# Smaller attention blocks, finer row work in the first search, and longer turns in the quantile stage of a graph-attention and quantile kernel

## The chip, the cores and the metric

The kernel runs on one core of one Trainium2 chip. The metric is the device time of one launch in microseconds (us), the median of several runs. Engines are named as in the profile: PE (TensorE), DVE (VectorE), ACT (ScalarE), POOL (GpSimd), SP (SyncE). PEld is PE's weight load.

## What is computed

Two layers over the same graph of 4096 nodes with 128 features each. `adj` is a 4096 x 4096 matrix of 0 and 1 with about 32 neighbours per row (11 to 55 with these inputs). The first layer is graph attention with eight heads, an output product, elu, a residual and a layer norm. The second takes, for each node, half of its neighbours by a rule on their positions, and of these the quantiles 0.25, 0.5 and 0.75 in each feature.

```python
# layer 0
Wh = jnp.einsum('nd,hde->hne', nodes, W)
f1 = jnp.einsum('hnd,hd->hn', Wh, a1)
f2 = jnp.einsum('hnd,hd->hn', Wh, a2)
e = jax.nn.leaky_relu(f1[:, :, None] + f2[:, None, :], negative_slope=ALPHA)
att = jnp.where(mask, e, jnp.float32(-9000000000000000.0))
att = jax.nn.softmax(att, axis=-1)
h = jax.nn.elu(jnp.einsum('hnm,hmd->hnd', att, Wh))
cat = jnp.transpose(h, (1, 0, 2)).reshape(N, NHEADS * DIM)
x = jax.nn.elu(cat @ W1 + b1)
out = _layernorm(nodes + x, gamma, beta)
# layer 1
m_i = jnp.where(num_nbr > T, jnp.ceil(num_nbr / K).astype(jnp.int32), jnp.int32(1))
remove = mask & ((rank + 1) % skip[:, None] == 0)
keep = mask & ~remove
svals = jnp.sort(jnp.where(keep[:, :, None], x[None, :, :], big), axis=1)
for q in QUANTILES:
    idx = jnp.maximum(jnp.ceil(q * n_keep).astype(jnp.int32) - 1, 0)
    agg = agg + w_q * jnp.take_along_axis(svals, idx[:, None, None], axis=1)[:, 0, :]
agg = (1.0 - SELF_RATIO) * agg + SELF_RATIO * x
out = agg @ W.T + b + x
```

## The kernel before

Rows are handled in 32 tiles of 128. The work has four stages that overlap.

*Search* (`neighbours`, L624 on). For each tile the adjacency row block is loaded (two halves of 1 MB, on ACT's DMA queue, L635), ACT takes its sign (L642), PE turns 512 columns at a time into keys that grow with the column's position (two products, L681 and L684), and DVE takes the eight largest keys of each 128 columns (L648). Eight such pieces make a tile. One tile later DVE selects the 64 largest of these, eight per piece (L653, L655). Groups of three or four tiles are then completed into records (`complete_records`): the neighbours' numbers, the count, the node's own number, its f1 terms and its features.

*Node rows* (`node_rows`, L542 on). Each node's features are transposed on PE (L585), copied by ACT (L587) and multiplied with the folded attention vectors `wa` (L579), which DVE makes from `W_sb` and `a_b` (L565, L568). The features with the f2 terms are stored as rows of `xt_d` in device memory. This generator runs inside the first search: each piece of the search is followed by one step of it.

*Attention*, in blocks of `BLOCKS` tiles (6, 10, 16). Once a block's tiles are searched, its rows are ordered by their number of neighbours (`rank_by_count`), their records are scattered in that order to `rec_d` (L228, tile name `rec_d`), and read back tile by tile (`read_lists`: R at L860, `narrow` at L886, both on SP's queue). So a tile holds rows of like size, and `CAPS` says how many neighbours a tile of a block needs. Its gathers are laid out in layers: of 32 neighbours for all rows, then of 16, 8 or 4 neighbours. `LAYERS` gives, for some tiles, layers that begin at a later row group (the third number), so that only the rows with most neighbours take part. Each gather is an indirect DMA of 128 rows of `xt_d` issued by POOL (L219, tile `G`); `G` has six buffers of 16 gathers. `attend` then adds f1 and f2 (L949), takes Exp on ACT (L956), makes denominators and their spread with PE (L964, L980), scales, spreads the weights (`wide`, L999) and sums the gathered rows with PE into `y` (L1012); then follow the head product (`hT`), elu, the output product (`small`), and the norm, whose result `x_t` is scattered to `x_d` by POOL. `TURNS` is the order of tiles in a block. While a block is attended, the next block's search runs in pieces between the steps of attention, `quota` of them per tile, spread evenly over all tiles but the last. In the last block, which has no search beside it, the records of all rows are also ordered over all tiles (`all_d`) and the lists of the second layer are made.

*Quantiles* (`quantile_out`, L1168 on). For each unit (one tile or two), POOL gathers the kept neighbours' rows of `x_d` into `vals` (L219, two buffers, one unit ahead), and DVE runs a network of minima and maxima over whole rows (L1225), keeping only the places that a quantile needs (`goal`); PE sums these with weights (L1244) and makes the output, which POOL scatters (L228, `out_dram`). Between network instructions DVE copies one word from PSUM to `junk` (L1196) to end what the code calls a turn; network instructions are cut so that a turn stays within `TURN_MIN`, `TURN_AIM` and `TURN_MAX`, in us by the model `TT_FIX + elements * TT_EACH`:

```python
if then(c * m) > TURN_MAX:
    room = int((TURN_AIM - then(0)) / (size * TT_EACH))
    if ran and room < 1:
        turn_of_gpsimd()
...
ran = then(c * m)
if ran > TURN_MIN:
    turn_of_gpsimd()
```

If a row doesn't fit its tile's bounds (`bad`), a general path at the end recomputes everything; it does not run with these inputs. The order of instructions on DVE, PE, ACT and POOL is that of the program and of its generators, moved only where the framework's fixed schedule brings later ready work forward.

Of the kernel before, what the change touches and what calls it, by code (L numbers as in the profile page):

```python
# [9 lines left out]
F32 = mybir.dt.float32  # L10
# [9 lines left out]
P = 128  # L20
N = 4096
D = 128
H = 8
NT = N // P
# [17 lines left out]


CAPS = {
    6: [28, 30, 33, 35, 39, 61],
    10: [26, 28, 30, 31, 33, 34, 36, 38, 40, 61],
    16: [24, 26, 28, 29, 30, 31, 31, 32, 33, 34, 35, 36, 38, 39, 42, 62],
    32: [
        23, 24, 25, 26, 27, 27, 28, 29, 29, 30, 30, 30, 31, 31, 32, 32,
        33, 33, 34, 34, 35, 35, 36, 36, 37, 37, 38, 39, 40, 41, 44, 63,  # L50
    ],
}
BLOCKS = [6, 10, 16]


LAYERS = {
    (6, 0): [(0, 16, 0), (16, 8, 0), (24, 4, 1)],
    (6, 2): [(0, 32, 0), (32, 8, 7)],
    (6, 5): [(0, 32, 0), (32, 16, 0), (48, 16, 15)],
    (10, 0): [(0, 16, 0), (16, 8, 0), (24, 4, 2)],  # L60
    (10, 4): [(0, 32, 0), (32, 32, 31)],
    (10, 7): [(0, 32, 0), (32, 4, 0), (36, 4, 2)],
    (10, 9): [(0, 32, 0), (32, 16, 0), (48, 16, 14)],
    (16, 14): [(0, 32, 0), (32, 8, 0), (40, 4, 2)],
    (16, 15): [(0, 32, 0), (32, 16, 0), (48, 16, 14)],
}


TURNS = {6: range(6), 10: range(10), 16: [0, 1, 2, 3, 15, 4, 5, 6, *range(8, 15), 7]}

CAP = CAPS[NT]
LOW = [
# [13 lines left out]


TT_FIX, TT_EACH, TT_OVER = 0.148, 0.001042, 0.077
TURN_MIN, TURN_AIM, TURN_MAX = 1.25, 1.45, 1.7


R_NUM, R_OWN, R_F1 = L, L + 1, L + 2
# [1 line left out]
R_X = R_F1 + H  # L94
# [8 lines left out]
def layers(c):  # L103


    out = []
    s = 0
    for w in (32, 32, 16, 8, 4):
        if (c + 3) // 4 * 4 - s >= w:
            out.append((s, w, 0))  # L110
            s += w
    return out
# [130 lines left out]
def kernel(  # L243
# [18 lines left out]
    xt_d = dram.tile([N + P, XW], F32, name="xt_d")  # L262
    recs_d = [dram.tile([n * P, REC], F32, name=f"rec{n}_d") for n in BLOCKS]
    all_d = dram.tile([N, REC1], F32, name="all_d")
# [35 lines left out]
    def search(t0, n):  # L300
        return neighbours(
            tc, adjp, cp, kp, rec, num, adj, t0, n, parts, markb, oneb, bad, jp1, pidx
        )

    with tc.tile_pool(name="setup", bufs=1) as sp, tc.tile_pool(
# [15 lines left out]
        )  # L321
        iota(nc, rowi, [[1, P]])
        rows = node_rows(tc, sp, pp, rec, x, W, W_sb, a1, a2, Wl, wa, WlT, ident, bad, xt_d)
        for i, _ in enumerate(search(0, BLOCKS[0])):
            if i > 0:
# [32 lines left out]
    def prepare(b, i, t0):  # L358
        n = BLOCKS[b]
        i = TURNS[n][i]  # L360
        parts = LAYERS.get((n, i)) or layers(CAPS[n][i])
        return read_lists(tc, attp, recs_d[b], i, CAPS[n][i], parts, t0 + i, bad, narrow, nodeq)

# [41 lines left out]
    def store_records(b, t0, ranks):  # L405

        return [
            (recs_d[b], rec[:, t0 + i, :], ranks[:, i : i + 1]) for i in range(BLOCKS[b])
        ]

    t0 = 0
    with tc.manual_schedule(engines=ORDERED):
        ranks = rank_by_count(tc, cp, kp, num, jp1, before, oneb, 0, BLOCKS[0])
        for v in store_records(0, 0, ranks):
# [22 lines left out]
        )  # L437
        for b, n in enumerate(BLOCKS):
            last = b == len(BLOCKS) - 1
# [102 lines left out]
def node_rows(tc, sp, pp, rec, x, W, W_sb, a1, a2, Wl, wa, WlT, ident, bad, xt_d):  # L542


    nc = tc.nc
    c = NT // 4
    load = nc.scalar.dma_start
    load(W_sb, W.rearrange("h d e -> d h e"))
    yield
    a_b = sp.tile([P, 2, H * D], F32, name="a_b")  # L550
    for i, a in enumerate((a1, a2)):
        load(a_b[:, i, :], a.rearrange("h d -> (h d)").partition_broadcast(P))
    wl_sb = sp.tile([P, D], F32, name="wl_sb")
    load(wl_sb, Wl)
    yield
    for i in range(4):
        for _ in range(3):
            yield
        load(
            rec[:, ts(i, c), R_X : R_X + D],  # L560
            x[ts(i, c * P), :].rearrange("(t p) d -> p t d", p=P),
        )
    for i in range(2):
        wprod = sp.tile([P, H, D], F32, name="wprod")
        nc.vector.tensor_tensor(  # L565
            wprod, W_sb, a_b[:, i, :].rearrange("p (h d) -> p h d", h=H), ALU.mult
        )
        nc.vector.tensor_reduce(wa[:, ts(i, H)], wprod, AX.X, ALU.add)  # L568
        yield
    F = sp.tile([P, NT, 2 * H], F32, name="F")  # L570
    xT = f_ps = None
    for t in range(0, NT + 8, 4):
        if f_ps is not None:
            nc.scalar.copy(F[:, t - 8 : t - 4, :], f_ps)
            f_ps = None
        if xT is not None:
            f_ps = pp.tile([P, 4, 2 * H], F32, name="f_ps")
            for u in range(4):
                nc.tensor.matmul(f_ps[:, u, :], lhsT=xT[:, ts(u, P)], rhs=wa, start=True, stop=True)  # L579
            xT = None  # L580
        yield
        if t < NT:
            xt_ps = pp.tile([P, 4 * P], F32, name="xt_ps")
            for u in range(4):
                nc.tensor.transpose(xt_ps[:, ts(u, P)], rec[:, t + u, R_X : R_X + D], ident)  # L585
            xT = sp.tile([P, 4 * P], F32, name="xT", bufs=2)
            nc.scalar.copy(xT, xt_ps)  # L587
        yield
    for dst, src in ((R_F1, F[:, :, 0:H]), (R_X + D, F[:, :, H:])):
        nc.vector.tensor_scalar(rec[:, :, dst : dst + H], src, FMAX, -FMAX, ALU.min, ALU.max)  # L590
    for i in range(4):
        nc.sync.dma_start(
            xt_d[ts(i, c * P), :].rearrange("(t p) w -> p t w", p=P),
            rec[:, ts(i, c), R_X:],
        )
    pad = sp.tile([P, XW], F32, name="pad")
    nc.gpsimd.memset(pad[:, 0:D], 0.0)
    nc.gpsimd.memset(pad[:, D:], PADF)
    nc.sync.dma_start(xt_d[N:, :], pad)
    yield  # L600
    sq = sp.tile([P, NT, 2 * H], F32, name="sq")
    nc.vector.tensor_tensor(sq, F, F, ALU.mult)
    fm = sp.tile([P, NT], F32, name="fm")
    nc.vector.tensor_reduce(fm, sq, AX.X, ALU.max)

    nc.vector.tensor_scalar(fm, fm, FMAX * FMAX, None, ALU.is_le)
    nc.vector.tensor_scalar(bad[:, 3, :], fm, -1.0, 1.0, ALU.mult, ALU.add)
    yield
    wl_ps = pp.tile([P, 4 * P], F32, name="xt_ps")[:, 0:D]
    nc.tensor.transpose(wl_ps, wl_sb, ident)  # L610
    nc.scalar.copy(WlT, wl_ps)
# [886 lines left out]
```

## Time and profile before

| what | us |
|---|---|
| median of 3 runs (lowest, highest) | 3615.5 (3614.76, 3617.49) |
| profiled execution | 3611.8 |
| its span | 3610.1 |
| first gather of rows (`G`) starts | 150.8 |
| last gather of rows starts | 1778.7 |
| first gather of `vals` starts | 1828.3 |
| first and last network instruction (L1225) start | 1857.3, 3596.3 |
| busy: PE, DVE, ACT, POOL | 1258, 2743, 400, 2344 |

Starts are from the profiled execution, counted from the span's start. In the slices of the page each digit is the busy share of a 40th of the span in tenths. POOL's busy time counts the 0.94 us of an indirect DMA and not the 0.30 us to the next one, so a full row of gathers shows as 7. A group's line gives the count, the busy time, the mean time of one, and the idle time of its engine just before it with what ended it.

### The profile page before, as it was taken

The numbers are of one execution on the slowest core, as the hardware profiler recorded it, in microseconds if no ns is written. First come the engines' busy times: TensorE is split into PE (matmuls) and PEld (weight loads), VectorE is DVE, ScalarE is ACT, GpSimd is POOL, SyncE is SP. The second block draws the span as 40 slices with busy tenths as digits, with TensorE's granted clock in tenths as the row PEclk, the third lists the DMA queues.
The fourth block names the chain that finished last, engine by engine and source line by source line (L and its number), as shares of the span: only waits on it lengthen the run. The fifth ranks groups of instructions, "written<-read, shape, count | busy, mean of one in ns | idle before, by whom it ended". The sixth has DMA issues, their size and how long they took to land. (4 is left out here: it accounts for less than half of the span.)

```text
span 3610.1 us, 22900 instructions
## 1 busy us (share of the span) xinstructions
PE 1258.1 (35%) x5323; PEld 951.4 (26%) x5323; DVE 2742.8 (76%) x7591; ACT 399.5 (11%) x555; POOL 2344.3 (65%) x2341
## 2 busy tenths in 40 slices
PE   6377667878456454456610000000000000001101
PEld 3044545445455454355510000000000000000101
DVE  7787548877345122157448999999999999999998
ACT  3122122322111011111110000000000000000000
POOL 1375767757777777777557776777555766667530
PEclk9965557566556555555555555555555555555555
DMA  6443244432222222222111111111111111111100
GB/s 212 132 147 90 67 149 139 142 123 70 59 63 55 55 55 54 66 58 55 43 38 48 48 47 41 46 47 46 39 34 37 47 44 40 43 45 47 38 20 3
DMA packets 109137, 237.46 MB, mean 66 GB/s; under 512 B 46720, under 2 KB 63104, under 8 KB 100800
## 3 DMA queue, kind: packets, MB, share of 16 engines
q0 software_dynamic: 74368, 156.34, 15.5%
q10 hardware_dynamic: 14848, 70.85, 5.7%
q1 hardware_dynamic: 19776, 8.73, 1.1%
q8 instruction: 44, 0.72, 0.1%
q14 instruction: 101, 0.83, 0.1%
HBM read 224.60 MB, written 11.15 MB: 65 GB/s over the span
## 5 line engine op out<-in xcount | busy, mean ns | idle before, releaser
L219 POOL DMA_INDIRECT G<-xt_d,idx x1124 | 1096.6, 976 | 416.3 <-issue 324.0
L219 POOL DMA_INDIRECT vals<-x_d,idx x1024 | 1052.3, 1028 | 333.9 <-issue 298.0
L1225 DVE TENSOR_TENSOR work<-work 128x512 f32<-128x512 f32 (+6 forms) x1405 | 959.4, 710 | 0.4
L1244 PE MATMUL st_ps<-dg,goal 128*128 128x128 f32 x286 | 71.8, 429 | 1644.7 <-DVE goal L1225 1574.6
L1225 DVE TENSOR_TENSOR work<-work,work 128x512 f32<-128x512 f32 (+5 forms) x958 | 604.9, 655 | 0.7
L1244 PEld LDWEIGHTS st_ps<-dg,goal 128*128 128x128 f32 x286 | 63.8, 324 | 1651.0 <-issue 1650.2
L1012 PE MATMUL y<-wide,G 128*128 128x32 f32 (+3 forms) x2248 | 482.7, 392 | 26.9 <-DVE wide L999 26.9
L1012 PEld LDWEIGHTS y<-wide,G 128*128 128x128 f32 x2248 | 461.2, 309 | 62.3 <-DVE wide L999 30.0
L648 DVE MAX8 first<-key 128x8 f32<-128x128 f32 x1024 | 225.2, 281 | 119.0 <-PE key L684 118.5
L949 DVE TENSOR_TENSOR z<-G,f1x 128x128 f32<-128x128 f32 (+5 forms) x92 | 29.0, 328 | 307.9 <-DMA G<-xt_d,idx 302.7
L228 POOL DMA_INDIRECT out_dram<-o,own_i x32 | 51.0, 1593 | 295.3 <-ACT o L1270 276.1
L681 PE MATMUL key<-sgn,markb 128*128 128x512 bf16 x256 | 149.3, 583 | 145.3 <-DVE first L648 98.2
L1196 DVE COPY junk<-still 128x1 f32<-128x1 f32 x1295 | 191.2, 148 | 0.0
L1225 DVE TENSOR_TENSOR work<-vals 128x1024 f32<-128x1024 f32 (+8 forms) x140 | 138.8, 1007 | 46.2 <-DMA vals<-x_d,idx 45.9
L642 ACT ACTIVATE sgn<-adj_t 128x2048 bf16<-128x2048 int32 x64 | 122.1, 1907 | 355.4 <-PE key L681 304.8
L1043 PE MATMUL small<-W_sb,late 128*128 128x128 f32 x512 | 126.0, 430 | 88.4 <-DVE late L1040 88.4
L1243 ACT ACTIVATE dg<-ident,wt 128x128 f32<-128x128 f32 x143 | 47.5, 393 | 955.9 <-PE st_ps L1244 955.6
L964 PE MATMUL small<-z,own 128*4 128x32 f32 (+6 forms) x438 | 49.6, 280 | 284.8 <-ACT z L956 284.8
L684 PE MATMUL key<-parts,oneb 64*128 64x512 bf16 x256 | 147.2, 575 | 0.2 <-POOL parts L237 0.2
L1043 PEld LDWEIGHTS small<-W_sb,late 128*128 128x128 f32 x512 | 111.7, 324 | 102.7 <-DVE late L1040 99.0
L980 PE MATMUL rz<-rden,ownT 4*128 4x32 f32 (+6 forms) x438 | 97.8, 386 | 78.0 <-DVE rden L975 63.0
L1031 PE MATMUL hT<-late,W_sb 128*128 128x128 f32 x512 | 110.9, 385 | 35.4 <-ACT late L1025 35.4
(184 smaller groups left out, 1763.3 us busy)
## 6 DMA issues: line engine op xcount, KB each, us to landing
adj_t<-in_adj_dram ACTq DMA_DIRECT2D x64, 1024.0 KB
G<-xt_d,idx POOLq DMA_INDIRECT x1124
vals<-x_d,idx POOLq DMA_INDIRECT x1024
R<-rec_d SPq DMA_DIRECT2D x128, 26.2 KB
xt_d<-rec SPq DMA_DIRECT2D x4, 544.0 KB
rec<-in_x_dram ACTq DMA_DIRECT2D x4, 512.0 KB
narrow<-rec_d SPq DMA_DIRECT2D x68, 5.2 KB
a_b<-in_L_gnn_a_dram ACTq DMA_DIRECT2D x2, 512.0 KB
```

Of the source, the lines that this page charges most:

```text
L219: nc.gpsimd.indirect_dma_start(out=dst, out_offset=None, in_=rows, in_offset=bass.IndirectOffsetOnAxis(ap=idx, axis=0),)
L642: nc.scalar.activation(sgn, adj_t, AF.Sign, accum_out=cnt[:, i : i + 1])
L648: nc.vector.max(first[:, ts(c0 // CW + c, 8)], key[:, ts(c, CW)])
L681: nc.tensor.matmul(key, lhsT=markb, rhs=sgn[:, ts(b, 512)], start=True, stop=False)
L684: nc.tensor.matmul(key, lhsT=oneb[0:64, :], rhs=parts[1][:, ts(r - 1, 512)] if r else parts[0], start=False, stop=True)
L980: nc.tensor.matmul(rz[:, layer[i] * H : (layer[i] + w - g0) * H], lhsT=ownT[w][:, r, :], rhs=rden.rearrange("p (g r h) -> p r g h", r=k // ...
L1012: nc.tensor.matmul(yf[:, ts(g, c)], lhsT=G[:, col + j - a, 0:D], rhs=pf[:, ts(j, c)], start=(i == 0 and g % (w // 2) == w // 2 - 1), stop= ...
L1031: nc.tensor.matmul(hT[:, ts(h, P)], lhsT=consts["W_sb"][:, h, :], rhs=yT[:, h, :], start=True, stop=True)
L1043: nc.tensor.matmul(o, lhsT=hv[:, h, :], rhs=consts["W1_sb"][:, h, :], start=(h == 0), stop=(h == H - 1))
L1196: nc.vector.tensor_copy(junk, late["still"])
L1225: nc.vector.tensor_tensor(slots_of(dst, (j, c, s, m), size), slots_of(a, (i, c, s, m), size), slots_of(b, (i + d, c, s, m), size), op,)
L1244: nc.tensor.matmul(st_ps[:, u, :], lhsT=goal[:, (j * k + u) * D : (j * k + u + 1) * D], rhs=dg, start=(j == 0), stop=False,)
```

## The change

There are three parts. (1) In the first search the node rows are done one tile per step: one transpose, one copy, and the product three steps later, instead of four transposes and four products in alternate steps; the loads of W and the attention vectors are issued some steps later. (2) The bounds of a turn in the quantile stage go from 1.25, 1.45 and 1.7 to 1.1, 1.9 and 2.4. (3) The blocks are 4, 6, 9 and 13 tiles instead of 6, 10 and 16, with caps, layers and an order of turns of their own. In the kernel after, the same lines have numbers that are 7 to 10 higher.

```diff
--- before.py
+++ after.py
@@ -42,31 +42,38 @@
 
 
 CAPS = {
+    4: [29, 33, 37, 60],
     6: [28, 30, 33, 35, 39, 61],
-    10: [26, 28, 30, 31, 33, 34, 36, 38, 40, 61],
-    16: [24, 26, 28, 29, 30, 31, 31, 32, 33, 34, 35, 36, 38, 39, 42, 62],
+    9: [26, 28, 30, 32, 33, 35, 37, 40, 61],
+    13: [25, 27, 28, 30, 31, 32, 33, 34, 35, 37, 39, 41, 62],
     32: [
         23, 24, 25, 26, 27, 27, 28, 29, 29, 30, 30, 30, 31, 31, 32, 32,
         33, 33, 34, 34, 35, 35, 36, 36, 37, 37, 38, 39, 40, 41, 44, 63,
     ],
 }
-BLOCKS = [6, 10, 16]
+BLOCKS = [4, 6, 9, 13]
 
 
 LAYERS = {
+    (4, 1): [(0, 32, 0), (32, 8, 7)],
+    (4, 2): [(0, 32, 0), (32, 4, 0), (36, 8, 7)],
+    (4, 3): [(0, 32, 0), (32, 16, 0), (48, 16, 15)],
     (6, 0): [(0, 16, 0), (16, 8, 0), (24, 4, 1)],
     (6, 2): [(0, 32, 0), (32, 8, 7)],
     (6, 5): [(0, 32, 0), (32, 16, 0), (48, 16, 15)],
-    (10, 0): [(0, 16, 0), (16, 8, 0), (24, 4, 2)],
-    (10, 4): [(0, 32, 0), (32, 32, 31)],
-    (10, 7): [(0, 32, 0), (32, 4, 0), (36, 4, 2)],
-    (10, 9): [(0, 32, 0), (32, 16, 0), (48, 16, 14)],
-    (16, 14): [(0, 32, 0), (32, 8, 0), (40, 4, 2)],
-    (16, 15): [(0, 32, 0), (32, 16, 0), (48, 16, 14)],
+    (9, 0): [(0, 16, 0), (16, 8, 0), (24, 4, 2)],
+    (9, 4): [(0, 32, 0), (32, 4, 1)],
+    (9, 6): [(0, 32, 0), (32, 4, 0), (36, 4, 2)],
+    (9, 8): [(0, 32, 0), (32, 16, 0), (48, 16, 14)],
+    (13, 0): [(0, 16, 0), (16, 8, 0), (24, 4, 3)],
+    (13, 6): [(0, 32, 0), (32, 4, 2)],
+    (13, 9): [(0, 32, 0), (32, 4, 0), (36, 4, 3)],
+    (13, 11): [(0, 32, 0), (32, 8, 0), (40, 4, 3)],
+    (13, 12): [(0, 32, 0), (32, 16, 0), (48, 16, 14)],
 }
 
 
-TURNS = {6: range(6), 10: range(10), 16: [0, 1, 2, 3, 15, 4, 5, 6, *range(8, 15), 7]}
+TURNS = {4: range(4), 6: range(6), 9: range(9), 13: [0, 1, 2, 3, 12, 4, 6, 7, 8, 9, 10, 11, 5]}
 
 CAP = CAPS[NT]
 LOW = [
@@ -86,7 +93,7 @@
 
 
 TT_FIX, TT_EACH, TT_OVER = 0.148, 0.001042, 0.077
-TURN_MIN, TURN_AIM, TURN_MAX = 1.25, 1.45, 1.7
+TURN_MIN, TURN_AIM, TURN_MAX = 1.1, 1.9, 2.4
 
 
 R_NUM, R_OWN, R_F1 = L, L + 1, L + 2
@@ -545,8 +552,11 @@
     nc = tc.nc
     c = NT // 4
     load = nc.scalar.dma_start
+    for _ in range(4):
+        yield
     load(W_sb, W.rearrange("h d e -> d h e"))
-    yield
+    for _ in range(2):
+        yield
     a_b = sp.tile([P, 2, H * D], F32, name="a_b")
     for i, a in enumerate((a1, a2)):
         load(a_b[:, i, :], a.rearrange("h d -> (h d)").partition_broadcast(P))
@@ -554,7 +564,7 @@
     load(wl_sb, Wl)
     yield
     for i in range(4):
-        for _ in range(3):
+        for _ in range(2):
             yield
         load(
             rec[:, ts(i, c), R_X : R_X + D],
@@ -568,24 +578,24 @@
         nc.vector.tensor_reduce(wa[:, ts(i, H)], wprod, AX.X, ALU.add)
         yield
     F = sp.tile([P, NT, 2 * H], F32, name="F")
-    xT = f_ps = None
-    for t in range(0, NT + 8, 4):
-        if f_ps is not None:
-            nc.scalar.copy(F[:, t - 8 : t - 4, :], f_ps)
-            f_ps = None
-        if xT is not None:
-            f_ps = pp.tile([P, 4, 2 * H], F32, name="f_ps")
-            for u in range(4):
-                nc.tensor.matmul(f_ps[:, u, :], lhsT=xT[:, ts(u, P)], rhs=wa, start=True, stop=True)
-            xT = None
+
+    LAG = 3
+    turned, f_ps = [], None
+    for t in range(NT + LAG):
+        if t < NT:
+            xt_ps = pp.tile([P, 4 * P], F32, name="xt_ps")[:, 0:P]
+            nc.tensor.transpose(xt_ps, rec[:, t, R_X : R_X + D], ident)
+            xT = sp.tile([P, P], F32, name="xT", bufs=LAG + 2)
+            nc.scalar.copy(xT, xt_ps)
+            turned.append(xT)
+        u = t - LAG
+        if u >= 0:
+            if u % 4 == 0:
+                f_ps = pp.tile([P, 4, 2 * H], F32, name="f_ps")
+            nc.tensor.matmul(f_ps[:, u % 4, :], lhsT=turned.pop(0), rhs=wa, start=True, stop=True)
         yield
-        if t < NT:
-            xt_ps = pp.tile([P, 4 * P], F32, name="xt_ps")
-            for u in range(4):
-                nc.tensor.transpose(xt_ps[:, ts(u, P)], rec[:, t + u, R_X : R_X + D], ident)
-            xT = sp.tile([P, 4 * P], F32, name="xT", bufs=2)
-            nc.scalar.copy(xT, xt_ps)
-        yield
+        if u > 0 and u % 4 == 3:
+            nc.scalar.copy(F[:, u - 3 : u + 1, :], f_ps)
     for dst, src in ((R_F1, F[:, :, 0:H]), (R_X + D, F[:, :, H:])):
         nc.vector.tensor_scalar(rec[:, :, dst : dst + H], src, FMAX, -FMAX, ALU.min, ALU.max)
     for i in range(4):
```

## The prediction

> **What bounds the kernel now.** I read the page first (busy shares, slices, costliest groups), then the stretches cut where the kernel changes stage, then the waits of VectorE inside the attention stage, then the order of time in the quantile stage. The chain that ended last holds only the final stores (0.7% of the span, "issue"), so it says nothing here.
>
> ```profile
> DVE  7787548877345122157448999999999999999998
> POOL 1375767757777777777557776777555766667530
> L219 POOL DMA_INDIRECT G<-xt_d,idx x1124 | 1096.6, 976 | 416.3 <-issue 324.0
> L219 POOL DMA_INDIRECT vals<-x_d,idx x1024 | 1052.3, 1028 | 333.9 <-issue 298.0
> L1196 DVE COPY junk<-still 128x1 f32<-128x1 f32 x1295 | 191.2, 148 | 0.0
> ```
>
> ```profile
> 120.00:150.80 30.80, 3.10 (x7) 0.69 (x7) 13.59 (x58) 0.00 (x0) 8.30 (x14) 1.00 0.09 27
> 150.80:476.70 325.90, 216.50 (x773) 135.60 (x773) 215.79 (x832) 65.49 (x68) 223.35 (x230) 0.60 0.37 112
> 476.70:1005.00 528.30, 382.28 (x1585) 261.38 (x1585) 363.51 (x1336) 126.52 (x133) 369.81 (x376) 0.60 0.37 111
> 1005.00:1781.00 776.00, 425.47 (x2097) 389.52 (x2097) 316.64 (x992) 104.16 (x112) 590.62 (x604) 0.55 0.22 57
> 1828.30:3610.00 1781.70, 125.97 (x542) 108.00 (x542) 1723.93 (x3944) 58.67 (x185) 1137.51 (x1088) 0.52 0.14 40
> ```
>
> Columns of the stretches: length, then busy time and count of PE, PEld, DVE, ACT, POOL. Two limits follow each other. Up to 1828 us it is POOL's row of gathers: a gather takes 0.944 us and the next starts 0.30 later, so 1.25 us each; POOL at "7" is full. In 1005 to 1781 it does 604 operations in 776 us, 1.285 each. In the two stretches before, 230 and 376 operations take 326 and 528 us: at 1.25 that leaves some 38 and 58 us in which POOL waits. From 1828 on DVE is the limit: 1724 of 1782 us.
>
> ```profile
> DVE bad L869 <- DMA R<-rec_d: 52.4, 3, 50.4
> DVE up L867 <- DMA R<-rec_d: 39.6, 2, 38.8
> ```
>
> These are VectorE's waits in attention: at each border between blocks it stands still once (50.4 and 38.8 us) until the next block's records are stored and read back, and the next search stands with it.
>
> ```profile
> 2500.05 0.41 DVE L1225 TENSOR_TENSOR work<-work,work 128x256 f32<-128x256 f32 x1
> 2500.32 0.96 POOL L219 DMA_INDIRECT vals<-x_d,idx  x1 [0.30 <-issue]
> 2500.39 0.14 DVE L1196 COPY junk<-still 128x1 f32<-128x1 f32 x1
> ...
> 2501.58 1.03 POOL L219 DMA_INDIRECT vals<-x_d,idx  x1 [0.30 <-issue]
> 2501.72 0.14 DVE L1196 COPY junk<-still 128x1 f32<-128x1 f32 x1
> 2501.79 0.94 DVE L1225 TENSOR_TENSOR work<-work 128x768 f32<-128x768 f32 x1
> 2502.66 0.41 DVE L1225 TENSOR_TENSOR work<-work,work 128x256 f32<-128x256 f32 x1
> ```
>
> Start to start, 768 elements take 0.87 us and 256 take 0.34: 1.04 ns per element and 0.07 per instruction; the copy also costs 0.07. Both gathers end 0.89 us after the copy begins that follows their start (2501.28 and 2502.61): a gather gets through when a DVE instruction gives way to the next.
>
> **What the Trainium skill says.** "SBUF — State Buffer", Who interferes with whom: a VectorE instruction with two SBUF inputs contends with a GpSimd one that reads SBUF, and the loser waits. The trace agrees: gathers lengthen only in the quantile stage (mean 1028 against 944 ns median in attention) and end in step with VectorE. "VectorE: DVE Perf Modes", the errata section: a fixed price per instruction, not a factor, and (N+151)/0.96 ns for an fp32 sum. The trace has 682 ns for 512, as that gives 691, but overlapped starts leave only 0.07 us of it per instruction; I use the trace.
>
> **The change part by part.**
>
> *Quantile pieces (longer turns).* Running the cutting rule of both kernels over the 21 units: the network's instructions go from 2649 (the page's groups of L1225 add up to this) to 2250, turns from 1295 to 1118; elements stay 1,382,784. Check of the prices: 1,382,784 x 1.042 ns + 3944 x 0.067 = 1705 us; the trace has 1739 from the first network instruction (1857.3) to the last (3596.4), 13.8 of it a wait. So 399 + 177 = 576 instructions at 0.067 go: -38.6. Against it stands POOL: a unit's turns cover the next unit's gathers. Before, 78 turns face 66 gathers and 2 stores; after, pairs have 59 for 68, 55 for 64, 50 for 60. A copy alone would no longer be enough, but borders between two network instructions let gathers through too (2309.36 is such a border: gather 2309.30 ends at 2310.26), `vals` is free after some 10% of a unit, and a wait costs only in the last units where the lead is used up. Laying each unit's gathers along its borders (one per border, starts at least 1.2 us apart) leaves some 4 us of waits; if only the copy and the instruction after it let POOL in, 22. So -34, between -17 and -39.
>
> *First search: 4 tiles, finer node rows.* Before, the first gather of rows starts at 150.8. Read from the order of time: a piece of the search costs 1.57 us (DVE), but 2.4 while four transposes and four products share PE (two pieces 4.79); the third sign pass is 5 us late behind the `a_b` and `wl` issues on ACT's queue (2.2 and 1.57); a tile is 8 pieces; the last tile's selection takes 7.8; bookkeeping and ranks 11 (116.0 to 127.1); six scatters 2.66 apart; 8.0 from the last to the first gather. After: pieces 0 to 7 end at 19 as now; the third sign stands ahead of the loads, so piece 15 ends at 33 (8 x 1.57, 1 of wait); two pieces and the four `wprod` instructions of 1.21, 41; 14 pieces with one transpose (0.23) and one product (0.43) beside 1.06 of key products on PE, 1.72 each, 65; last selection 74; bookkeeping 11, plus 2.3 for the clamps and squares now queued on DVE ahead of the ranks, ranks at 88. Of the 35 row steps 25 fall into the search; the last 10, 0.7 each on PE, delay the ranks' products by 1 or 2 us, taken in. Four scatters instead of six: 2 x 2.66 less. First gather at 107: -43, give or take 8. ScalarE's 32 copies in place of 8 cost nothing while it idles (0.3 us each beside 1.72). The stores of `xt_d` (2.2 MB on SP's queue, ahead of the R reads) move to 84; at the 113 to 321 GB/s of the first stretches they take 7 to 20 us and 23 are there; if slower, the first gather moves with them, up to 10.
>
> *Blocks 4, 6, 9, 13 with own partial layers.* Gathers per block: before 217 + 351 + 556 = 1124, after 151 + 217 + 317 + 451 = 1136; 12 x 1.25 = +15. Two more `rec_d` scatters lie in POOL's row (28 against 26): +2.6. Bookkeeping of DVE per layer follows the lists, 66 to 71, at about 1.2 us, beside gathers. What remains is POOL's waiting: 1630 us from 150.8 to 1781 against 1211 operations at 1.285, 74 us. I walk through the new blocks with the steps that the trace shows: the Exp passes are 54.7 us apart with 20 pieces per step and 48.7 with 17, so 15 + 2 per piece; a tile's G buffers are free 36 us after its Exp (27 to 38 seen); six buffers of 16 columns. Block of 4: 21 pieces per step, Exps at 145, 202, 259; POOL reaches the fourth tile at 237 and ends near 307. Border 10 us as at 467 to 477 before. Block of 6 (18 pieces): Exps from 383 every 51; POOL waits 7, 6 and 24 us for buffers, ends near 648. Border 10. Block of 9 (16 pieces): Exps from 718 every 47; waits of 9, 16 and 21, end 1126. Last block from 1134: 451 + 32 + 13 = 496 operations at 1.285, 1771 against 1781. So the 43 us from the start shrink to -10: 18 for more operations, the rest for a third border and its buffer waits. I take -8, between -59 (waiting 40 in all) and +50. The 47 us from there to the first `vals` gather stay.
>
> **Sum.** -34 - 8 = -42. The profiled execution took 3611.8 (span 3610.1), so 3570; the median of the runs is 3.7 higher, 3615.5, so 3573.5.
>
> **The rivals.**
> - *The search no longer holds back POOL.* For: per block, steps of search are fewer per gather (62 pieces for 151, 89 for 217, 124 for 317; before 97 for 217 and 148 for 351). Waiting 40 instead of my 94: -43 + 18 - 34 = -59, with the quantiles -93: 3522. Against: 21 pieces in a step of 41 us of gathers is more than now.
> - *The longer pieces starve the gathers.* A piece of 2048 elements holds off a gather for 2.2 us; 59 turns do not serve 68. Only 17 of 38 remain: 3615.5 - 17 - 8 = 3590. Against: gathers seen ending at plain borders.
> - *The third border eats it all (slower).* POOL's 74 us of waiting over two borders are 37 each; if each of three costs 50, because the searches of 9 and 13 tiles start only after VectorE's standstill of 39 to 50 us and hold the buffers, the attention is -43 + 18 + (150 - 74) = +51; with -34, 3632. It decides from 44 per border on (132 in all). For: the two waits shown. Against: a smaller block's waits for buffers are fewer.
> - *The change does not do what it says*: a tile whose neighbours overflow its layers would start the general path. Sorting the rows' neighbour counts of these inputs (11 to 55) into the new blocks, no row exceeds its layers; left out.
>
> **How the numbers follow.** Forecast (3574, its own range 3550 to 3595) 45%; search no longer holding back (3522) 20%; starved gathers (3590) 15%; third border (3632) 13%; 7% for mixtures near 3615. Range 3518 to 3622. A measurement of this kernel tells about 0.2% (7 us) from no change. Faster: 45 + 20 + 15 and little of the mixtures, 0.80; same 0.06; slower 0.14.
>
> **What would show it.** Right: the first gather of rows near 107; the first `vals` gather 0 to 30 us earlier than 1828; 1118 copies on `junk`, 2250 network instructions, the stage from first to last network instruction near 1705; waits of VectorE for `vals` at 46 to 55. Wrong: `vals` waits of 20 us in the units of two tiles; a first gather later than 120, with PE or the `xt_d` stores before it; three standstills of VectorE for R of 50 us and buffer waits of POOL over 100.

## The result, and the profile after

The changed kernel takes 3564.1 us (median of 4 runs, 3558.6 to 3568.0), the kernel before 3615.1 beside it: ratio 0.9861, 95% interval 0.9842 to 0.9881. The forecast was 3574. The profiled execution spans 3556.4 us against 3610.1, so 53.7 less, and these divide at the first `vals` gather:

| step (us) | before | predicted | after |
|---|---|---|---|
| ranks of the first block done | 127.1 | 88 | 83.3 |
| first gather of rows (`G`) | 150.8 | 107 | 103.2 |
| block ends (last gather) | 467, 1004, 1780 | 307, 648, 1126, 1771 | 302.1, 636.0, 1115.0, 1764.9 |
| gap in the row of gathers between blocks | 9.3, 4.1 | 10, 10, 8 | 1.6, 6.2, 4.5 |
| first `vals` gather | 1828.3 | 1820 | 1813.3 |
| from there to the end of the span | 1781.8 | 1748 | 1743.1 |
| first to last network instruction | 1739.3 | 1705 | 1699.5 |
| VectorE's waits for `vals` | 45.9 | 50 | 48.1 |

So 15.0 us come from attention and what stands ahead of it, 38.7 from the quantile stage. These are readings of one execution of each kernel, and that of the changed kernel was the fastest of its four; the medians lie 51.0 apart.

The page of the changed kernel, the slices of DVE and POOL and three groups (count, busy time, mean of one, idle time before it):

```profile
DVE  7783774477761522248538999999999999999998
POOL 1676757676677777777647777788777688777771
...
L226 POOL DMA_INDIRECT vals<-x_d,idx x1024 | 1220.8, 1192 | 316.4 <-issue 309.4
L226 POOL DMA_INDIRECT G<-xt_d,idx x1136 | 1107.7, 975 | 440.6 <-issue 329.3
...
L1206 DVE COPY junk<-still 128x1 f32<-128x1 f32 x1118 | 168.3, 151 | 0.0
```

POOL's row is full one slice earlier (the 6 in the second slice, where before had 3); DVE's row of nines begins in the same slice as before. The gathers of `vals` became longer (1192 ns, before 1028): 1024 x 0.164 = 168 us more busy time on POOL, and almost none of it arrives at VectorE, as the waits below show. What holds a gather off is seen in the order of time of the changed kernel (start, duration, engine, line, operation):

```profile
2500.23 1.23 POOL L226 DMA_INDIRECT vals<-x_d,idx  x1 [0.30 <-issue]
2500.57 0.15 DVE L1206 COPY junk<-still 128x1 f32<-128x1 f32 x1
...
2501.77 1.57 POOL L226 DMA_INDIRECT vals<-x_d,idx  x1 [0.30 <-issue]
2502.44 0.15 DVE L1206 COPY junk<-still 128x1 f32<-128x1 f32 x1
```

The two gathers end at 2501.46 and 2503.34, 0.89 and 0.90 us after the start of the copy. Of the 514 gathers in the stage that took over 1 us, 485 end within 0.87 to 0.93 us after a copy starts, and 14 after a network instruction starts.

The stretches of the changed kernel, cut at its stages (length, then busy time and count of PE, PEld, DVE, ACT, POOL, then clock, DMA share, GB/s):

```profile
80.00:103.20 23.20, 2.65 (x6) 0.59 (x6) 9.39 (x31) 0.00 (x0) 6.38 (x12) 1.00 0.43 125
103.20:303.00 199.80, 116.73 (x439) 70.83 (x440) 129.67 (x512) 33.86 (x35) 151.90 (x158) 0.80 0.36 97
303.00:637.00 334.00, 234.33 (x931) 160.48 (x931) 214.66 (x799) 74.82 (x78) 223.83 (x232) 0.57 0.38 110
637.00:1126.00 489.00, 346.43 (x1459) 242.80 (x1458) 322.77 (x1182) 112.51 (x118) 339.29 (x346) 0.59 0.38 109
1126.00:1770.00 644.00, 346.41 (x1815) 317.50 (x1816) 278.16 (x906) 83.48 (x90) 481.81 (x491) 0.57 0.24 56
1813.30:3556.40 1743.10, 124.38 (x542) 106.69 (x542) 1681.97 (x3368) 58.82 (x185) 1306.45 (x1088) 0.52 0.16 41
```

POOL does 158 + 232 + 346 + 491 = 1227 operations between its first gather (103.2) and the end of the last one (1764.9). At the 1.285 us of the prediction that is 1577 of 1662 us, so it waits 85 us in all (forecast 94, before 74). In the last stretch VectorE has 3368 instructions in place of 3944, and is busy for 1682 of 1743 us.

The waits of the changed kernel (in total, times, longest):

```profile
DVE z L959 <- DMA G<-xt_d,idx: 235.9, 22, 31.4
DVE up L877 <- DMA R<-rec_d: 118.0, 4, 48.7
...
POOL G L226 <- PE y L1022: 93.6, 13, 25.4
...
DVE work L1235 <- DMA vals<-x_d,idx: 48.1, 2, 32.5
```

And POOL's wait for buffers in the kernel before:

```profile
POOL G L219 <- PE y L1012: 70.4, 10, 30.2
```

VectorE stands still for R three times now (28.5, 40.0 and 48.7 us; before 38.8 and 50.4), one border more. During these three standstills POOL issued 22, 31 and 38 gathers and scatters, with no pause over 0.31 us between two of them. POOL's waits for free `G` buffers grew by 23 us. The waits for `vals` are still the two of the ramp (the start of the stage, where the gathers have no lead yet), 32.5 and 15.6, in the first two units; none came in the later units.

The two runs above and e8 below ran on chips where the kernel before takes 3609 to 3615 us (the first kind); e1 to e4, e6, e7 and e9 ran on chips where the same program takes 4534 to 4593 (what the traces show of this stands in the last section). So those runs are read as ratios to the kernel before on the same chip, and their times aren't set beside 3564.

### The profile page after: what moved, and what is told of

It reads as the page before. It is cut to its first block, busy times and chain, and to the rows that moved or that the text cites. A ratio compares the mean times of both kernels' runs of the same rounds, so it can differ in the third digit from the quotient of the medians.

```text
span 3556.4 us, 22742 instructions
## 1 busy us (share of the span) xinstructions
PE 1251.8 (35%) x5474; PEld 948.3 (27%) x5474; DVE 2716.1 (76%) x7111; ACT 403.3 (11%) x579; POOL 2523.4 (71%) x2353
## 5 line engine op out<-in xcount | busy, mean ns | idle before, releaser
L226 POOL DMA_INDIRECT vals<-x_d,idx x1024 | 1220.8, 1192 | 316.4 <-issue 309.4
L226 POOL DMA_INDIRECT G<-xt_d,idx x1136 | 1107.7, 975 | 440.6 <-issue 329.3
L1235 DVE TENSOR_TENSOR work<-work 128x512 f32<-128x512 f32 (+7 forms) x1194 | 933.5, 811 | 0.6
L1235 DVE TENSOR_TENSOR work<-work,work 128x512 f32<-128x512 f32 (+6 forms) x821 | 590.4, 740 | 0.5
L959 DVE TENSOR_TENSOR z<-G,f1x 128x128 f32<-128x128 f32 (+4 forms) x97 | 29.1, 319 | 237.6 <-DMA G<-xt_d,idx 235.9
L1235 DVE TENSOR_TENSOR work<-vals 128x1536 f32<-128x1536 f32 (+7 forms) x96 | 133.4, 1405 | 48.5 <-DMA vals<-x_d,idx 48.1
L1206 DVE COPY junk<-still 128x1 f32<-128x1 f32 x1118 | 168.3, 151 | 0.0
```

The source lines that it names most:

```text
L226: nc.gpsimd.indirect_dma_start(out=dst, out_offset=None, in_=rows, in_offset=bass.IndirectOffsetOnAxis(ap=idx, axis=0),)
L1206: nc.vector.tensor_copy(junk, late["still"])
L1235: nc.vector.tensor_tensor(slots_of(dst, (j, c, s, m), size), slots_of(a, (i, c, s, m), size), slots_of(b, (i + d, c, s, m), size), op,)
```

## The experiments

The theory: in the quantile stage each instruction of VectorE that goes saves its start of 0.067 us, and gathers still get through in time, since they pass at any border between two instructions; in attention POOL's row of gathers sets the time, so it gains what it starts earlier, less what it waits more. Rivals: the copies alone let gathers through; the standstills at the borders set the time.

| run | us | before beside it | ratio, 95% interval |
|---|---|---|---|
| e1_turns | 4314.1 | 4550.4 | 0.9506 [0.9466, 0.9546] |
| e2_rows | 4537.0 | 4550.4 | 0.9989 [0.9958, 1.002] |
| e3_blocks | 4565.9 | 4550.4 | 1.0054 [1.0016, 1.0092] |
| e4_nocopy | 4322.4 (one run) | 4550.4 | |
| e6_fill | 4351.7 | 4593.4 | 0.9475 [0.9411, 0.9539] |
| e7_after | 4326.4 | 4550.0 | 0.9507 [0.9469, 0.9544] |
| e7_turns | 4320.0 | 4550.0 | 0.9506 [0.9464, 0.9549] |
| e7_attn | 4539.9 | 4550.0 | 0.9979 [0.9955, 1.0004] |
| e7_nocopy | 4332.4 | 4550.0 | 0.9547 [0.951, 0.9584] |
| e8_double | 3770.0 | 3609.0 | 1.0449 [1.0429, 1.047] |
| e8_long | 3564.0 | 3609.0 | 0.9875 [0.9858, 0.9891] |
| e9_fill | 4327.5 | 4534.0 | 0.9538 [0.9507, 0.957] |

**The longer turns alone (e1_turns, and again as e7_turns).** The kernel before with one line changed:

```diff
-TURN_MIN, TURN_AIM, TURN_MAX = 1.25, 1.45, 1.7
+TURN_MIN, TURN_AIM, TURN_MAX = 1.1, 1.9, 2.4
```

> The kernel before with only the three turn bounds changed to 1.1, 1.9, 2.4. Theory (576 fewer VectorE instructions at 0.067 to 0.071 us each, gathers not starved): 3615 - 39 = 3576, VectorE's waits for vals unchanged near 46. Rival (the longer pieces starve the gathers, and the gain of the whole change came from the attention): 3615 - 17 = 3598 with waits for vals near 68.

> The kernel before with the long quantile pieces alone (bounds 1.1, 1.9, 2.4). Theory of the prediction (0.067 us for each of 576 instructions, waits for vals about the same): -38 of 3615, 3577, ratio 0.989, first vals unchanged at 1828. Rival (each instruction costs more than its start, as runs on the chips at 4550 suggest, 236 us for 576): where before takes 4550, 4314 again, ratio 0.951.

The ratio is 0.9506 both times. That is more than the forecast for this part, 1% of 3615: on these chips 576 fewer instructions save 230 to 236 us. The size is of these chips (the last section divides it), but the sign and the place are the theory's, and VectorE's waits for `vals` didn't grow: in front of instructions that read `vals` it stands 42.3 and 41.6 us in the two runs, against 45.9 in the kernel before on the first kind of chip.

**Finer rows alone, small blocks alone (e2_rows, e3_blocks).** The first is the kernel before with the new node rows and later loads in the first search, of which the core is

```diff
-    for t in range(0, NT + 8, 4):
+    for t in range(NT + LAG):
...
-            for u in range(4):
-                nc.tensor.transpose(xt_ps[:, ts(u, P)], rec[:, t + u, R_X : R_X + D], ident)
+            nc.tensor.transpose(xt_ps, rec[:, t, R_X : R_X + D], ident)
```

The second is the kernel before with

```diff
-BLOCKS = [6, 10, 16]
+BLOCKS = [4, 6, 9, 13]
```

and the caps, layers and order of turns that belong to these blocks.

> The kernel before with only the finer node rows in its first search of six tiles. Theory: the late third sign pass (5 us) goes and 35 row steps at 0.15 us over a piece replace 16 at 0.83, so the first gather of rows moves from 150.8 to about 138 and the time to 3602, as the attention after it has the same work. Rival (the buffer waits of the attention swallow an earlier start): first gather 138, time 3612 to 3615.

> The kernel before with only the blocks of 4, 6, 9 and 13, their caps, layers and turns; node rows and turn bounds as before. Theory: all row work fits into 42 steps at the old pace, first gather of rows near 113; the attention then takes the 1663 us from first gather to last that the changed kernel shows, 33 more than before, so about 3610. Rival (the smaller blocks themselves are what gained): 3600 or less. Rival (a third border costs more than the shorter first search brings): above 3620.

The first gather of rows came at 138.1 with the finer rows alone and at 112.7 with the small blocks alone, where 138 and 113 were expected. On these chips it comes at 149.0 and 149.4 with the old rows and blocks (e7_turns, e1_turns) and at 102.2 with both parts (e7_after). So of the 47 us by which the gathers start earlier, the finer rows give 11 alone, the smaller first block 36 alone, and they add. The totals show no gain from either: 0.9989 is no change, and 1.0054 is slower by 7 to 42 us. On these chips POOL waits 660 and 715 us for `G` buffers that PE hasn't finished with (70 and 94 on the others), so a start that comes earlier can be lost there; that it is lost in these waits was not tried apart.

**The parts beside the whole on one chip (e7_after, e7_attn).** The changed kernel, and the changed kernel with the old turns:

```diff
-TURN_MIN, TURN_AIM, TURN_MAX = 1.1, 1.9, 2.4
+TURN_MIN, TURN_AIM, TURN_MAX = 1.25, 1.45, 1.7
```

> The changed kernel itself, as the anchor for the runs beside it. On a chip that runs the kernel before at 3615: 3564 (ratio 0.986), attention up to the first vals gather 1813, network 1700. On a chip that runs the kernel before near 4550, the quantile part alone gave 0.951 and the two attention parts 0.999 and 1.005: if they add, 0.951 + 0.004 = 0.955 (4345); if finer rows and small blocks help each other (a smaller first block starts only because the rows come finer), 0.945 or below.

> The change without the long quantile pieces (bounds 1.25, 1.45, 1.7). If the parts add: 3615 - 15 = 3600, ratio 0.996, first vals at 1813, network 1739. Where before takes 4550: 1.004 if the attention parts add (0.999 and 1.005), 0.996 or below if they help each other.

The whole has 0.9507, the turns alone 0.9506, and the attention parts alone 0.9979, which is -10 us with an interval from -20 to +2. So on these chips the turns are the whole of the gain that can be told; in their traces the first `vals` gather comes no earlier with the new attention (2491.7 and 2496.6 in e7_attn and e7_after) than with the old (2475.1 in e7_turns). The 15 us of attention are seen on the other chips only: the first `vals` gather at 1813.3 after the change, and at 1814.4 and 1813.9 in e8_double and e8_long, whose attention is the same, against 1828.3 before (one profiled execution). No run on those chips has the rows or the blocks alone. Rows and blocks together (0.9979) came out a little under the product of the two alone (1.0043); the intervals just touch and the chips differ, so that they help each other isn't shown.

**Without the copies (e4_nocopy, and again as e7_nocopy).** The changed kernel with

```diff
-        nc.vector.tensor_copy(junk, late["still"])
+        pass
```

> The changed kernel with the 1118 copies to junk left out, network instructions unchanged (the same output). Theory (a gather gets through at any border between two VectorE instructions, and the copy only adds a second border 0.07 us later that catches a gather that came just too late): VectorE saves 1118 x 0.07 = 75 us, gathers that miss a border wait for a whole further piece, VectorE waits some 230 us for vals in the units of two tiles, total about 3670. Rival (only the copy opens the way for POOL): gathers pass only when VectorE is idle, 900 of them at 1.25 us one after another with the network, over 4400. Rival (copies not needed at all): 3490.

> The changed kernel without its 1118 copies on junk. Theory (a gather passes at any border of VectorE's instructions, and copies give only more borders): 1118 x 0.067 = 75 us go, and waits for vals grow by as much or more: network stage 1700 to 1810, that is 3564 to 3675 where before takes 3615; 4320 to 4350 where it takes 4550. Rival (the copies are pure cost now that pieces are long): 3490, ratio 0.965 where before takes 3615; 80 under the changed kernel elsewhere.

The ratio 0.9547 lies 0.4% over that of the changed kernel (0.9507), the intervals overlap: taking out 1118 instructions gains nothing. In e7_nocopy VectorE stands 154 us in front of instructions that read `vals`, in e7_after 36. So 118 us of waits stand against the 75 us of the copies and some 47 us of other standstills that these chips have (last section): 13 to 24 us of waiting in each of the last six units, which begin 85 to 101 us apart. How gathers pass without copies is in the order of time of e7_nocopy (start, duration, engine, line, operation, count):

```profile
3978.59 1.81 DVE L1235 TENSOR_TENSOR work<-work,work 128x1024 f32<-128x1024 f32 x2
3979.19 1.43 POOL L226 DMA_INDIRECT vals<-x_d,idx  x1 [0.30 <-issue]
3980.33 1.81 DVE L1235 TENSOR_TENSOR work<-work 128x1024 f32<-128x1024 f32 x2
3980.92 1.43 POOL L226 DMA_INDIRECT vals<-x_d,idx  x1 [0.30 <-issue]
3982.07 1.81 DVE L1235 TENSOR_TENSOR work<-work,work 128x1024 f32<-128x1024 f32 x2
3982.66 1.43 POOL L226 DMA_INDIRECT vals<-x_d,idx  x1 [0.30 <-issue]
```

A line marked x2 holds two network instructions; the second one of the first line starts at 3979.72 in the trace, and the gather ends 0.90 after that, at 3980.62. There is no copy in this kernel, so it passed at the border between two network instructions. Of the 599 gathers that took over 1 us, 546 end 0.87 to 0.93 us after the start of a network instruction. From gather to gather it is 1.73 us here in place of 1.25. So the rival that only a copy lets a gather through falls, and so does the other one, that the copies are pure cost: on these chips they are worth about what they cost. The kernel without copies has no run on the first kind of chip.

**Each copy twice (e8_double).**

```diff
         nc.vector.tensor_copy(junk, late["still"])
+        nc.vector.tensor_copy(junk, late["still"])
```

> The changed kernel with each of its 1118 copies on junk made twice. The prediction prices an instruction of VectorE in the quantile stage at its start alone, 0.067 us: +75 us, 3639 where before takes 3615 (ratio 1.007), 4400 where before takes 4550 (0.968), waits for vals no longer than before. Rival (on the chips that take 4550 for before an instruction costs 0.40 us, as 231 us for 576 fewer suggest): +447, 4773, ratio 1.049.

Neither number came. It fell on a chip with 3609 for before; the time was 3770.0, and the span is 211.4 over that of the changed kernel: 0.19 us per added copy. The order of time of e8_double, VectorE alone:

```profile
2501.31 0.15 DVE L1206 COPY junk<-still 128x1 f32<-128x1 f32 x1
2501.49 0.16 DVE L1207 COPY junk<-still 128x1 f32<-128x1 f32 x1
2501.57 0.42 DVE L1236 TENSOR_TENSOR work<-work 128x256 f32<-128x256 f32 x1
2501.90 0.42 DVE L1236 TENSOR_TENSOR work<-work,work 128x256 f32<-128x256 f32 x1
...
2503.37 0.15 DVE L1206 COPY junk<-still 128x1 f32<-128x1 f32 x1
2503.55 0.16 DVE L1207 COPY junk<-still 128x1 f32<-128x1 f32 x1
```

From the first copy to the second it is 0.18 us (median of the 1118 pairs 0.185), from the second copy to the network instruction 0.08. The second copy starts 0.03 after the end of the first, where a network instruction starts 0.08 before the end of the copy ahead of it. The trace points to a reason: all 1118 second copies carry a wait for the semaphore (a counter to wait on) that VectorE's own instructions count up, and none of the network instructions behind them does. Of the first copies 1029 carry it too and still start 0.08 before the end of the instruction ahead, so it is for something older there; the start of the second copies fits a wait for the first copy to be finished. Both write the same tile, which would explain that; the awaited count isn't in the trace, and a second tile wasn't tried. The Trainium skill, "Perfetto Trace Analysis", in the part DVE / Act Engine Instruction, says that the recorded time of an instruction runs until its bytes are acknowledged, and that the next one may begin to read its data before that; a start 0.08 before the recorded end, where nothing is waited for, agrees with that. So this run doesn't measure the price of an independent instruction, and the 0.067 rests on the distance from start to start in the trace and on the 40 us that the change itself saved.

**Still longer turns (e8_long).**

```diff
-TURN_MIN, TURN_AIM, TURN_MAX = 1.1, 1.9, 2.4
+TURN_MIN, TURN_AIM, TURN_MAX = 1.1, 2.8, 3.4
```

> The changed kernel with still longer pieces (bounds 1.1, 2.8, 3.4): 37 network instructions and 35 copies fewer. Laying the gathers along VectorE's borders: 5 us go, waits for vals rise from 48 to 89, so +36 us: 3600 where before takes 3615; 4360 where it takes 4550 (0.958). Rival (fewer instructions always pay, at 0.40 us on these chips): -29 us, 4297, ratio 0.944.

3564.0, ratio 0.9875 [0.9858, 0.9891], beside 0.9861 [0.9842, 0.9881] of the change: no difference that can be told, and not the 36 us of loss that laying the gathers along the borders gave. The waits of e8_long:

```profile
DVE work L1235 <- DMA vals<-x_d,idx: 48.4, 3, 32.4
...
DVE work L1235 <- issue: 8.2, 1, 8.2
```

Here a wait of 8.2 us, with two of half a microsecond, came in three of the last units, where 41 us more waiting was expected. So laying the gathers along the borders overstates the waits, but the first late ones do show. They outweigh the 5 us of the 72 instructions that went: from first to last network instruction it is 1704.1 us, 4.6 more than in the changed kernel.

**Search into the standstills (e6_fill, and again as e9_fill).** The changed kernel with pieces of the next search, 16 and 22, put ahead of the wait for R:

```diff
+FILL = [0, 16, 22]
...
+            if not last:
+                for _ in range(FILL[b]):
+                    next(pieces, None)
+                    left -= 1
             ready.append(prepare(b, 0, t0))
```

> The changed kernel with part of the next search issued on VectorE ahead of the wait for the new block's records: 16 pieces at the border from 4 to 6 tiles, 22 at that from 6 to 9 (none at the first and the last); the steps of those blocks then carry 15 and 13 pieces instead of 18 and 16. Theory (VectorE's standstills of 28 and 40 us at the borders delay the searches, and the lag is what makes POOL wait 41 and 48 us in the blocks of 6 and 9): those waits shrink to under 20 each and the time falls by 50 to 80 us against the changed kernel (on the chip of the first profiles 3485 to 3515; 0.965 to 0.972 of the kernel before). Rival (POOL's waits come from the length of one tile's chain of engines, not from VectorE's load): less than 15 us.

> The changed kernel with 16 and 22 pieces of the next search put into the standstills of VectorE (28.5 and 40.0 us) in front of the blocks of 6 and 9 tiles, where it waits for R. Theory of the third border (standstills push the searches late, which hold buffers): waits for R fall from 118 to about 55 and the blocks of 6 and 9 end 10 to 25 us earlier, 3540 to 3555 where before takes 3610 (ratio 0.981 to 0.985). Rival (the prediction: the row of gathers sets the time, a standstill is hidden by it): waits for R fall all the same, time within 5 us of 3564 (0.987). Second rival (the pieces stand in front of what the border waits for): borders of 29 and 39 us in POOL's row as on the chips that take 4550, and 3580 to 3600.

Both fell on chips of the 4534 to 4593 kind: 0.9475 and 0.9538, on both sides of the 0.9507 of the changed kernel on a third chip, so neither a gain nor a loss is shown. POOL's gaps at the first two borders became 29 and 40 to 42 us in both (in e7_after 7.6 and 5.9), and the blocks of 6 and 9 tiles became 25 to 31 us shorter: what the fill takes at the border it gives back inside the block. Whether it pays where VectorE does stand still for 28.5 and 40.0 us stays open.

## Why the prediction was right

**The quantile stage: -34 forecast, -38.7 measured.** The counts came as the cutting rule gave them (2250 network instructions, 1118 copies). From first to last network instruction, without the one wait in it (13.8 before, 15.6 after), it is 41.6 us for 576 instructions: 0.072 each, priced at 0.067. With 0.072 the price check of the prediction, which had left 20 us open (1705 against 1739 less the wait of 13.8), closes for both kernels: 1725 and 1683 us, measured 1725.5 and 1683.9. The 4 us of waits set against the gain were 2.2. That the gathers become late was the rival "the longer pieces starve the gathers"; they did become longer, by 0.164 us each, but POOL's row had that much room.

Where the gathers pass isn't quite what the forecast leaned on. It feared too few turns in the units of two tiles and counted on the borders between two network instructions. In the last nine of these units 516 gathers were issued while 515 copies ran, and all but 8 of them passed in front of a copy or just behind one. For that case the prediction had reckoned 22 us of waits; so its 4 us came near with another way of passing than the one it counted on, which is in part luck. The borders between network instructions do carry gathers where there are no copies (e7_nocopy).

The skill ("SBUF — State Buffer", Who interferes with whom) says that a VectorE instruction with two SBUF inputs contends with a GpSimd instruction that reads SBUF. The traces here limit what that costs: a gather that is held off mostly ends 0.90 us after the next border. The prediction's comparison beside it set a mean against a median; mean against mean, a gather took 1028 ns in the quantile stage and 976 in attention, where 65 of 1124 took over 1.1 us too. e7_nocopy shows how near the edge is: fewer borders than now, and waits take back all that is saved.

**The start: first gather at 107 forecast, 103.2 measured.** Ranks came at 83.3 in place of 88, the rest of the way took 19.9 in place of 19. e2_rows and e3_blocks put the two shares where they were expected (138.1 and 112.7).

**Attention: -8 forecast, -15.0 measured.** The sign was right and POOL's row did set the time, but the size is partly luck, as two terms were off against each other. The borders were set at 10, 10 and 8 us, after one of the two seen before; they measured 1.6, 6.2 and 4.5, 16 us less. The blocks were set at 200, 331, 468 and 637 us from first to last gather; they measured 198.8, 332.3, 472.8 and 645.5, 13 more, most of it in the last block. The Exps of the first block came at 145.7, 200.4 and 248.2 where 145, 202 and 259 were written. The waiting of 94 us that the prediction names doesn't follow from its own row: from 107 to 1771, 1664 us, less 1225 operations at 1.285, leaves 90; 85 were measured. The 47 us from the last block to the first `vals` gather stayed (48.4).

**The rivals.** "The third border eats it all" had its premise come true, three standstills of VectorE of up to 48.7 us, and not its conclusion: POOL goes on gathering through them, and its row has gaps of 1.6 to 6.2 there. Its waits for buffers, the other way in which a standstill could reach the end, grew by 23 us, and all its waiting by 11 to 85; the rival needed 150. "The search no longer holds back POOL" needed 40 us of waiting; there are 85.

## What to carry to other kernels

When an engine is full with many instructions, count the instructions: at 0.07 us from start to start 576 of them were 40 us, with the elements unchanged, and the trace before the change had both numbers. Before making an engine's turns longer, lay the work of the engine that must squeeze in along the remaining borders unit by unit. What matters isn't how much each transfer lengthens but whether the unit with the least room still ends in time; in e8_long this found the units where the first waits come, but not their size (41 us expected, 9 measured). A standstill of one engine at a border says nothing until the row of the engine that sets the time shows a gap there too.

## What the runs showed of the hardware

**Two copies in a row on one tile are 0.185 us apart, not 0.07.** The second one carries a wait for VectorE's own semaphore and starts 0.034 us after the recorded end of the first. So a price per instruction that is read from pairs in which the second needn't wait for the first doesn't hold for a pair in which it must.

**The same program took 3564 us on one chip and 4326 on another.** The instructions last equally long (the `junk` copy 151 and 150 ns, the `G` gather 975 and 960); it is the starts that are late. In e2_rows, in the order of time of the quantile stage:

```profile
3343.66 0.94 POOL L219 DMA_INDIRECT vals<-x_d,idx  x1 [0.30 <-issue]
3344.91 0.95 POOL L219 DMA_INDIRECT vals<-x_d,idx  x1 [0.30 <-issue]
3345.38 0.16 DVE L1199 COPY junk<-still 128x1 f32<-128x1 f32 x1 [2.84 <-remote]
3345.45 1.28 DVE L1228 TENSOR_TENSOR work<-work 128x512 f32<-128x512 f32 x2
...
3349.58 0.16 DVE L1199 COPY junk<-still 128x1 f32<-128x1 f32 x1 [2.84 <-remote]
3349.66 1.22 DVE L1228 TENSOR_TENSOR work<-work 128x1024 f32<-128x1024 f32 x1
```

VectorE stands for 2.84 us in front of a copy, while POOL goes on at 1.25 us per gather. There are 143 such gaps over 0.3 us in that stage, 113 of them in front of a copy, 330 us in all with the one wait for the first `vals` (32.0); the changed kernel on the first chip has 2, both waits for `vals`, 48.1 us in all. Of 131 starts after a gap that follow another within 12 us, 128 follow it at a multiple of 0.70 us, to within 0.03 (here 4.20 = 6 x 0.70). The gaps come in clusters; one stretch of 1091 VectorE instructions has none.

What the instructions after a gap have in common is a wait. In 138 of the 143 gaps the next instruction waits for VectorE's own semaphore alone, the one that its earlier instructions count up, and in front of instructions without any wait there are 2, of 1.7 us together. Only 1567 of the 3944 instructions carry a wait for that semaphore, 1202 of the 1295 copies among them. The waits in e2_rows (in total, times, longest):

```profile
DVE junk L1199 <- remote: 100.9, 41, 3.5
DVE junk L1199 <- DVE work L1228: 71.2, 60, 2.2
```

So on these chips VectorE often goes on late after a wait for itself, with all its earlier instructions ended. This speaks against a late delivery of instructions, which should also show in front of those that wait for nothing. In attention it shows as waits of other engines. The longest of e7_after:

```profile
POOL G L226 <- PE y L1022: 724.6, 33, 43.3
...
ACT late L1047 <- remote: 594.1, 21, 47.3
DVE rden L984 <- remote: 423.8, 14, 72.8
```

It also divides the larger gain of the turns there, 230 us for 576 instructions. From e7_attn to e7_after the way from first to last network instruction shortens by 235 us (2031.3 to 1796.0). The gaps in front of waits for VectorE's own semaphore fall from 289 to 97 us, so 192 of these; the 43 that remain are what the same 576 instructions saved on the first kind of chip (41.6). So an instruction's own price isn't higher there; what falls is the number of these standstills, from 136 to 43. In e7_nocopy they are 18, 50 us in all, but there the waits for `vals` grew.

What makes these waits end late isn't settled. The traces of these chips hold only half of the semaphore records (24,116 updates against 48,504 for the same program), so that "remote" there may be a releaser whose record is missing.
